# A four-layer graph network on one core: inverse norms brought back interleaved, diagonal blocks summed on VectorE, another order of the first loads

## The chip, the cores and the metric

The kernel runs on one core of a Trainium2 chip. The metric is the device time in microseconds (us) from the first to the last instruction of that core. The core has TensorE (PE, matrix products), VectorE (DVE), ScalarE (ACT), GpSimd (POOL) and SyncE (SP, which here issues nearly all DMA transfers). Each engine works through its own instructions in order; the engines wait for each other by semaphores.

## The reference, cut to what matters

There are 32 graphs (batches) of 512 nodes with 128 features, each with its own 512 x 512 weighted adjacency. Four layers follow each other, each on the normed nodes, each added to its input:

```python
h = relu(layernorm(x))
# layer 0: (adj + eye) scaled on both sides by degree ** -0.5
adj1 = adj + eye(512);  r = sum(adj1, -1) ** -0.5
x = x + leaky_relu((adj1 * r[:, :, None] * r[:, None, :]) @ (h @ W) + b)
# layer 1: adj @ elu(in), adj.T @ elu(out), elu(node), one update with tanh
# layer 2: four steps, each of them
src_agg = einsum('bjv,bij->biv', nodes @ ws + bs, l2norm(adj, 2))   # by rows of adj
dst_agg = einsum('bjv,bji->biv', nodes @ wd + bd, l2norm(adj, 1))   # by columns of adj
nodes = tanh(concat(src_agg, nodes @ wn + bn, dst_agg) @ wu + bu)   # steps 2, 3 also take earlier nodes
# layer 3: a gated recurrent unit on m = tanh(adj @ msg)
```

Everything is float32. The host lays `adj` and its transpose out by partition (`adj`, `adjt`), so that the kernel holds `a` and `aT`, each 128 partitions x 4 chunks x 512.

## The kernel before

The kernel does not issue its instructions as it meets them. It records every operation with its engine, an assumed duration and the buffers it reads and writes, and a planner (`Plan`) then lays them out in one fixed order for each engine, interleaving two or three batches, and assigns buffers from pools. Where the planner expects a hole in PE's work, it puts in small products (`ps_idle`) that keep PE's clock up; their results are not used. A line in the profile such as L350 is a helper that records matmuls, so its rows are told apart by tile names.

Loads wait in the planner as long as data is on a round trip through DRAM (`plan.way` opens at the first operation and closes at the last): "loads yield to turned rows". Only what stands in `FIRST` is exempt, and is issued in that order:

```python
TURN = 32
OWN = 2
FIRST = ["x0", "a0", "aT0", "c", "raw0", "w1", "r1", "raw2", "raw3", "x1", "a1", "aT1", "x2", "a2", "aT2"]
...
        def load(dst, src, kb, rank):
            name = f"{rank}{b}"
            rank, kb = first(name), kb * (2 if name == "a0" else 1)
            n = NC // pieces
            for k in range(pieces):
                s = slice(k * n, (k + 1) * n)
                op("SP", 0.4, lambda s=s: nc.sync.dma_start(dst.ap()[:, s, :], src[:, s, :]),
                   [], [(dst, set(range(NC)[s]))], kb=kb / pieces, rank=rank, yields=rank is None)
```

`raw0`, `raw2`, `raw3` are layer 2's raw weights, which the kernel multiplies into one another (`ps_fold`) before it uses them; `c` holds biases.

Layer 0 adds the unit matrix to the four diagonal 128 x 128 blocks of `aT`, into `diag`; the aggregation then takes `diag` for those blocks and `aT` for the rest. The sum is one instruction over all four blocks (one for each block in batch 0):

```python
        n = NC if b else 1
        own_engine, own_name = (nc.vector, "DVE") if b < OWN else (nc.gpsimd, "POOL")
        for k in range(0, NC, n):
            op(own_name, t_tt(n * P) if b < OWN else t_pool(n * P), lambda k=k, n=n: own(k, n), [(aT, set(range(k, k + n))), ID], [(diag, set(range(k, k + n)))])
```

Layer 2 needs each row and column of the adjacency divided by its norm. ACT sums squares along the free dimension into `stat` (128 x 8: four chunks of `a`, four of `aT`), POOL raises them to the power -0.5, and the 8 x 128 results must then stand along the free dimension, the same on all partitions, to be multiplied into `aT` and `a`:

```python
        root = op("POOL", t_pow(2 * NC), lambda: nc.gpsimd.tensor_tensor(inv.ap()[:, :2 * NC], stat.ap(), neg_half, op=ALU.pow), [stat, NH], [inv])
        bounce, rows = buf("bounce", (P, TURN)), buf("s4", (P, NC, 2, NC, TURN), "rows")
        op("DVE", 0.1, lambda: nc.vector.transpose(turned_inv.ap(), inv.ap()), [inv], [turned_inv])
        # bounced(): 128 x 32 from turned_inv to DRAM
        # spread():  from DRAM to all partitions, 4 runs of 256 words each
        op("SP", 0.4, bounced, [turned_inv], [bounce], kb=16)
        plan.way(root, op("SP", 0.4, spread, [bounce], [rows], kb=640))
        for s, m in enumerate((aT, a)):
            for c in range(NC):
                op("DVE", t_tt(N), lambda m=m, c=c, s=s: nc.vector.tensor_mul(
                    m.ap()[:, c, :].rearrange("p (k q r) -> p k q r", k=NC, q=NC), m.ap()[:, c, :].rearrange("p (k q r) -> p k q r", k=NC, q=NC),
                    rows.ap()[:, :, s].rearrange("p q c r -> p c q r")), [(m, {c}), rows], [(m, {c})])
```

The same DVE turning of 32 x 32 blocks, with a trip through DRAM (`turn_turned`, `turned`, `f4r`), turns node rows into columns in the middle batches; batches 0, 1 and 31 use PE for it.

Other names that the prediction uses: `h` is the normed node tile (four ACT ACTIVATEs), `hT` and `f` have features on partitions, `rep` holds layer 1's `elu` of `in` and `out`, `sd` layer 2's `src` and `dst` rows, `msg` layer 3's messages.

Of the kernel before, what the change touches and what calls it, by code (L numbers as in the profile page):

```python
# [13 lines left out]
F32 = mybir.dt.float32  # L14
AF = mybir.ActivationFunctionType
ALU = mybir.AluOpType
AX = mybir.AxisListType

P = 128
B, N, D = 32, 512, 128  # L20
NC = N // P
# [3 lines left out]
PERIOD = 28.0  # L25
ENDING = 6.0
SMALL = 16
TURN = 32
OWN = 2

FIRST = ["x0", "a0", "aT0", "c", "raw0", "w1", "r1", "raw2", "raw3", "x1", "a1", "aT1", "x2", "a2", "aT2"]


SEVEN = {"last": 0 * 5 * D, "mid": 1 * 5 * D, "gates": 2 * 5 * D}
# [242 lines left out]
def gnn_stack(  # L277
# [11 lines left out]
    nc = tc.nc  # L289
    const = ctx.enter_context(tc.tile_pool(name="const", bufs=1))  # L290
    sb = ctx.enter_context(tc.tile_pool(name="sb", bufs=1))
    psum = ctx.enter_context(tc.tile_pool(name="psum", bufs=1, space=bass.MemoryType.PSUM))
    dram = ctx.enter_context(tc.tile_pool(name="dram", bufs=1, space=bass.MemoryType.DRAM))
    plan = Plan(sb, psum, {"bank": 8, "s2": 33, "s4": 5, "s8": 10}, {"bank": 1, "s2": 5, "s4": 0, "s8": 1})

    w_sb = const.tile([P, W_COLS], F32, name="w_sb")
    c_sb = const.tile([P, C_COLS], F32, name="c_sb")
# [3 lines left out]
    t_sb = const.tile([P, T_COLS], F32, name="t_sb")  # L301
    cg_sb = const.tile([P, 4], F32, name="cg_sb")
    ident = const.tile([P, P], F32, name="ident")
    inv_sb = const.tile([P, 8, TURN], F32, name="inv_sb")
    neg_half = const.tile([P, 2 * NC], F32, name="neg_half")

    def wt(col, n=D):
# [9 lines left out]
    def t_tt(n, pointers=0):  # L317
        return 0.065 + 0.058 * pointers + n / 960
# [10 lines left out]
    def t_pow(n):  # L329
        return 0.35 + 0.157 * n  # L330

    def op(*args, **kwargs):
        return plan.op(*args, **kwargs)

    def first(name):
        return FIRST.index(name) if name in FIRST else None

    def const_buf(name, ap):
        b = Buf(plan, name, name, None)
        b.tile, b.slot = ap, 0  # L340
        return b

    W1, W2F, W3, CS, RS, RF, CF, TS, ID, NH, CG = (const_buf(n, t) for n, t in (
        ("w1", w_sb), ("w2", w_sb), ("w3", w_sb), ("c_sb", c_sb), ("r_sb", r_sb), ("rf_sb", rf_sb),
        ("cf_sb", cf_sb), ("t_sb", t_sb), ("ident", ident), ("neg_half", neg_half), ("cg_sb", cg_sb)))

    INV, INV_T = ([const_buf(f"inv{j}_{k}", inv_sb[:, 4 * j + k, :]) for k in range(4)] for j in range(2))

    def mm(ps, out_of, lhs, rhs, n, start, stop, reads, later=0.0):
        op("PE", t_mm(n), lambda: nc.tensor.matmul(out_of(ps.ap()), lhs(), rhs(), start=start, stop=stop),  # L350
           reads, [ps], later=later)
# [9 lines left out]
    def setup():  # L361
# [1 line left out]

        op("POOL", 1.0, lambda: make_identity(nc, ident), [], [ID])
        op("POOL", 0.2, lambda: nc.gpsimd.memset(neg_half, -0.5), [], [NH])
        op("POOL", 0.21, lambda: nc.gpsimd.memset(inv_sb, 0.0), [], INV + INV_T)
        first_l2 = W_L2[0][0]

        def spread(lo, hi, to=None):
# [21 lines left out]
        for i in (0, 2, 3):  # L391
            lo, hi = RAW_L2[i][0], RAW_L2[i + 1][0] if i == 2 else RAW_COLS if i == 3 else RAW_L2[2][0]
            buf = plan.buf("s8", (P, NC, N), f"raw{i}")
# [9 lines left out]
        for i, (k, (proj, upd)) in enumerate(zip(L2_CHUNKS, RAW_L2, strict=True)):  # L403
            part = [0, 2] * k + [1] * k
            buf = raws[i][0]
            for lo in range(0, 3 * k, NC):
                n = min(NC, 3 * k - lo)
# [41 lines left out]
    def program(b):  # L449
        plan.batch = b  # L450

        def buf(tag, shape=(P, N), name=None):
            return plan.buf(tag, shape, name)
# [68 lines left out]
        pieces = NC if b == 0 else 2  # L522

        def load(dst, src, kb, rank):


            name = f"{rank}{b}"
            rank, kb = first(name), kb * (2 if name == "a0" else 1)
            n = NC // pieces
            for k in range(pieces):  # L530
                s = slice(k * n, (k + 1) * n)
                op("SP", 0.4, lambda s=s: nc.sync.dma_start(dst.ap()[:, s, :], src[:, s, :]),
                   [], [(dst, set(range(NC)[s]))], kb=kb / pieces, rank=rank, yields=rank is None)
# [236 lines left out]
# [4 lines that stand above are left out]
        psh = plan.bank("agg")  # L774
# [17 lines left out]
        x1 = buf("s2", rows_shape, "xr")  # L792
# [3 lines left out]
        h1, _ = normed(x1, "h")  # L796
# [11 lines left out]
        for h in range(2):  # L808
            s, part, halves = slice(2 * h, 2 * h + 2), {2 * h, 2 * h + 1}, set(range(4 * h, 4 * h + 4))
# [19 lines left out]
        x2 = buf("s2", rows_shape, "xr")  # L829
# [3 lines left out]
        stat = buf("stat2", (P, 2 * NC))  # L833
        sq = buf("s2", name="sq")
        for c in range(NC):
            for s, m in ((0, a), (1, aT)):
                op("ACT", 0.73, lambda c=c, s=s, m=m: nc.scalar.activation(  # L837
                    sq.ap(), m.ap()[:, c, :], AF.Square, accum_out=stat.ap()[:, s * NC + c:s * NC + c + 1]), [(m, {c})], [sq, (stat, {s * NC + c})])
        inv, turned_inv = INV[b % len(INV)], INV_T[b % len(INV_T)]
        op("DVE", 0.08, lambda: nc.vector.tensor_scalar_max(stat.ap(), stat.ap(), NORM_EPS * NORM_EPS), [stat], [stat])  # L840
        root = op("POOL", t_pow(2 * NC), lambda: nc.gpsimd.tensor_tensor(inv.ap()[:, :2 * NC], stat.ap(), neg_half, op=ALU.pow), [stat, NH], [inv])  # L841


        bounce, rows = buf("bounce", (P, TURN)), buf("s4", (P, NC, 2, NC, TURN), "rows")
        op("DVE", 0.1, lambda: nc.vector.transpose(turned_inv.ap(), inv.ap()), [inv], [turned_inv])

        def bounced():
            bounce.tile = dram.tile([P, TURN], F32, name=f"bounce_{b}", tag=f"bounce_{bounce.slot}", bufs=1)
            nc.sync.dma_start(bounce.tile, turned_inv.ap())

        def spread():
            d = bounce.tile
            nc.sync.dma_start(rows.ap().rearrange("p q s c r -> p q (s c r)"),
                              bass.AP(tensor=d.tensor, offset=d.offset, ap=[[0, P], [TURN * TURN, NC], [1, 2 * P]]))

        op("SP", 0.4, bounced, [turned_inv], [bounce], kb=16)

        plan.way(root, op("SP", 0.4, spread, [bounce], [rows], kb=640))
        for s, m in enumerate((aT, a)):
            for c in range(NC):  # L860
                op("DVE", t_tt(N), lambda m=m, c=c, s=s: nc.vector.tensor_mul(  # L861
                    m.ap()[:, c, :].rearrange("p (k q r) -> p k q r", k=NC, q=NC), m.ap()[:, c, :].rearrange("p (k q r) -> p k q r", k=NC, q=NC),
                    rows.ap()[:, :, s].rearrange("p q c r -> p c q r")), [(m, {c}), rows], [(m, {c})])


        h2, _ = normed(x2, "h")
        f0 = transposed(h2, "f0")
        f, stashed = [f0], [f0]
# [4 lines left out]
        for i, (wsd, wn) in enumerate(W_L2):  # L873
# [11 lines left out]
            for h, o in order:  # L885
                m, lo = ((aT, 0), (a, D))[o]
# [10 lines left out]
            f = {0: [f_new], 1: [f_new, stashed[1]], 2: [f_new, stashed[1], stashed[0]], 3: [f_new]}[i]  # L897
# [14 lines left out]
        h3, _ = normed(x3, "h")  # L912
# [6 lines left out]
        aT2 = buf("s8", (P, NC, N), "aT2")  # L919
# [40 lines left out]
        u, n, q, w, xo = (buf("s2", rows_shape, k) for k in ("u", "n", "q", "w", "xo"))  # L960
        side, side_engine = (nc.gpsimd, "POOL") if at_end else (nc.vector, "DVE")
        w1 = 1 if at_end else 2
        for k in range(0, NC, w1):
            s, part, cols = slice(k, k + w1), set(range(k, k + w1)), 2 * D * w1
# [3 lines left out]
        for k in range(0, NC, w2):  # L968
            s, part, cols = slice(k, k + w2), set(range(k, k + w2)), w2 * D
# [71 lines left out]
```

## Time and profile before

| | before |
|---|---|
| device time, median of 3 runs | 2325.16 us (2324.03 to 2326.28) |
| span of the profiled run | 2322.2 us |
| busy: PE, DVE, ACT, POOL | 2301.4, 1529.8, 870.7, 261.8 us |
| granted PE clock | 1.000 |
| moved by DMA | 201.23 MB, 87 GB/s on average |

In the profile's rows, a group is one line, engine, operation and tile; after the bar stand its busy time, the mean duration of one instruction in ns, and the idle time of the engine ahead of the group with what ended it. Each float32 product is shown as two matmul records (two passes). Ends of matmuls are modelled, and successive matmuls overlap.

### The profile page before, as it was taken

How to read it: one execution, taken by the hardware profiler on the slowest of the kernel's cores; microseconds unless marked ns; L12 is line 12 of the kernel's file. 1: busy time of each engine (PE TensorE's matmuls, PEld its weight loads, DVE VectorE, ACT ScalarE, POOL GpSimd, SP SyncE). 2: the span in 40 equal slices, each digit the busy share in tenths (PEclk: the TensorE clock that was granted, in tenths of full speed). 3: DMA queues.
4: the chain of work that ended last, by engine and by line, in shares of the span. 5: the costliest groups of instructions: out<-in, count | busy, mean ns of one | idle time of the engine just before them, and what ended most of it. 6: DMA issues, size and time to landing. Idle time of an engine off the chain costs nothing.

```text
span 2322.2 us, 28292 instructions
## 1 busy us (share of the span) xinstructions
PE 2301.4 (99%) x9662; PEld 1442.0 (62%) x9662; DVE 1529.8 (66%) x4179; ACT 870.7 (37%) x1970; POOL 261.8 (11%) x210
## 2 busy tenths in 40 slices
PE   9999999999999999999999999999999999999999
PEld 7566666666666666666666656666666666566666
DVE  7646666676666766667666667666676666676655
ACT  7313433343333443334433334333344333343322
POOL 3001110111101111101101011110111110111101
PEclk9999999999999999999999999999999999999999
DMA  7102312323223323233232232322332222323201
GB/s 261 28 28 64 121 56 87 109 87 105 64 83 99 110 82 87 69 91 109 83 102 62 83 109 87 105 64 82 100 110 82 87 68 93 109 83 105 69 10 32
DMA packets 145056, 201.23 MB, mean 87 GB/s; under 512 B 18960, under 2 KB 96016, under 8 KB 144912
## 3 DMA queue, kind: packets, MB, share of 16 engines
q1 hardware_dynamic: 144624, 199.30, 27.9%
q8 instruction: 76, 1.25, 0.2%
q14 instruction: 68, 0.56, 0.1%
q10 hardware_dynamic: 288, 0.13, 0.0%
HBM read 160.05 MB, written 39.32 MB: 86 GB/s over the span
## 4 chain that ended last, share of the span: by engine, by line
PE 73%; DMA 10%; DVE 8%; POOL 3%; SPq 3%; ACT 2%; issue 1%; ACTq 0%; POOLq 0%; DVEq 0%
PE ps_agg L350 49%; PE ps_seven L716 9%; PE ps_sd L350 8%; DMA x<-in_x 4%; DMA turn_turned<-blk 3%; PE ps_gate L350 3%; PE ps_upd L350 2%; POOL sc L584 2%; SPq L614 2%; DVE bn L542 2%; PE ps_lin L350 1%; ACT h L596 1%; DVE sd L672 1%; POOL inv_sb L841 1%; DVE aT L861 1%
## 5 line engine op out<-in xcount | busy, mean ns | idle before, releaser
L350 PE MATMUL ps_agg<-aT,sd 128*128 128x512 f32 x1024 | 503.8, 593 | 0.1
L350 PE MATMUL ps_agg<-a,sd 128*128 128x512 f32 x1024 | 502.0, 593 | 0.0
L584 POOL TENSOR_TENSOR sc<-v,neg_half 128x4 f32<-128x4 f32 (+1 forms) x127 | 163.1, 1284 | 981.9 <-DVE v L759 489.9
L596 ACT ACTIVATE h<-xr,nb,sc 128x128 f32<-128x128 f32 x384 | 158.2, 482 | 277.3 <-DVE nb L592 277.2
L350 PEld LDWEIGHTS ps_agg<-aT,sd 128*128 128x128 f32 x1024 | 179.8, 191 | 109.6 <-issue 96.1
L350 PEld LDWEIGHTS ps_agg<-a,sd 128*128 128x128 f32 x1024 | 175.9, 191 | 114.8 <-issue 112.9
L350 PE MATMUL ps_agg<-f,w_sb 128*128 128x512 f32 x448 | 229.0, 593 | 0.4 <-ACT f L891 0.4
L716 PEld LDWEIGHTS ps_seven<-t_sb,s 128*128 128x128 f32 x1128 | 167.3, 191 | 92.6 <-issue 84.9
L350 PE MATMUL ps_sd<-w_sb,f 128*128 128x256 f32 x768 | 219.5, 380 | 0.5 <-ACT f L891 0.3
L965 ACT ACTIVATE g<-g 128x512 f32<-128x512 f32 (+1 forms) x64 | 36.1, 609 | 396.3 <-DVE g L694 395.8
L350 PEld LDWEIGHTS ps_sd<-w_sb,f 128*128 128x128 f32 x768 | 132.8, 191 | 79.8 <-issue 51.5
L716 PE MATMUL ps_seven<-t_sb,s 128*128 128x128 f32 x1128 | 178.6, 275 | 0.0
L672 DVE TENSOR_TENSOR sd<-ps_sd,rf_sb 128x512 f32<-128x512 f32 x128 | 87.8, 686 | 97.6 <-PE ps_sd L350 97.5
L742 DVE TENSOR_TENSOR ev<-ps_seven,ev 128x512 f32<-128x512 f32 x94 | 64.9, 691 | 131.7 <-PE ps_seven L716 131.4
L350 PE MATMUL ps_agg<-aT,msg 128*128 128x512 f32 (+1 forms) x264 | 132.0, 585 | 5.8 <-DVE msg L917 5.7
L350 PE MATMUL ps_agg<-aT,rep 128*128 128x512 f32 x256 | 131.0, 593 | 3.2 <-DVE rep L813 3.2
L350 PE MATMUL ps_agg<-a,rep 128*128 128x512 f32 x256 | 130.7, 592 | 0.0
L841 POOL TENSOR_TENSOR inv_sb<-stat,neg_half 128x8 f32<-128x8 f32 x32 | 53.0, 1657 | 672.3 <-DVE stat L840 648.8
L891 ACT ACTIVATE f<-ps_agg,cf_sb 128x512 f32<-128x512 f32 x128 | 87.3, 682 | 103.3 <-PE ps_agg L350 100.8
L716 PEld LDWEIGHTS ps_seven<-w_sb,f 128*128 128x128 f32 x512 | 80.4, 191 | 50.2 <-issue 47.3
L350 PE MATMUL ps_agg<-aT,h 128*128 128x256 f32 (+2 forms) x384 | 99.6, 381 | 0.6 <-ACT h L569 0.6
L837 ACT ACTIVATE sq<-aT 128x512 f32<-128x512 f32 x128 | 80.1, 626 | 51.0 <-DMA aT<-in_adjt 49.9
(175 smaller groups left out, 3781.0 us busy)
## 6 DMA issues: line engine op xcount, KB each, us to landing
aT<-in_adjt SPq DMA_DIRECT2D x124, 512.0 KB, 6.7
a<-in_adj SPq DMA_DIRECT2D x62, 512.0 KB, 5.7
turn_turned<-blk SPq DMA_DIRECT2D x348, 64.0 KB, 2.3
turned<-turn_turned SPq DMA_DIRECT2D x87, 256.0 KB, 2.7
rows<-bounce SPq DMA_DIRECT2D x32, 512.0 KB, 5.1
x<-in_x SPq DMA_DIRECT2D x32, 256.0 KB, 6.9
out<-xo SPq DMA_DIRECT2D x30, 256.0 KB, 2.0
turn_f4r<-blk SPq DMA_DIRECT2D x116, 64.0 KB, 1.8
```

The costliest lines, as they stand in the source:

```text
L350: op("PE", t_mm(n), lambda: nc.tensor.matmul(out_of(ps.ap()), lhs(), rhs(), start=start, stop=stop), reads, [ps], later=later)
L542: op("DVE", 0.193, lambda c=c: nc.vector.bn_stats(st.ap()[:, c, :], xin.ap()[:, c, :]), [xin], [(st, {c})])
L584: op("POOL", t_pow(n), lambda: nc.gpsimd.tensor_tensor(inv.ap()[:, :n], v8.ap()[:, :n], neg_half[:, :n], op=ALU.pow), [v8, NH], [(inv, {0})])
L596: op("ACT", t_act(D, 2), lambda c=c: nc.scalar.activation(h.ap()[:, c, :], xin.ap()[:, c, :], AF.Relu, bias=nb.ap()[:, c:c + 1], scale=inv ...
L614: nc.sync.dma_start(bounce.tile[:, k, :].rearrange("(b s) n -> s b n", b=NC), blk.ap()[k * P // NC:(k + 1) * P // NC])
L672: op("DVE", t_tt(N), lambda ps=ps, h=h: nc.vector.tensor_add(sd.ap()[:, 2 * h:2 * h + 2, :], ps.ap().rearrange("p (j v) -> p j v", j=2), s ...
L716: op("PE", t_mm(D), lambda j=j: nc.tensor.matmul(ps.ap()[:, k * H + j * D:k * H + (j + 1) * D], lhs()[:, j * P:(j + 1) * P], rhs(), start= ...
L742: op("DVE", t_tt(N), lambda: nc.vector.tensor_add(ev.ap(), bank_b.ap()[:, None, :H].to_broadcast([P, 2, H]), ev.ap()), [bank_b, ev], [ev])
L837: op("ACT", 0.73, lambda c=c, s=s, m=m: nc.scalar.activation(sq.ap(), m.ap()[:, c, :], AF.Square, accum_out=stat.ap()[:, s * NC + c:s * NC ...
L841: root = op("POOL", t_pow(2 * NC), lambda: nc.gpsimd.tensor_tensor(inv.ap()[:, :2 * NC], stat.ap(), neg_half, op=ALU.pow), [stat, NH], [inv])
L891: op("ACT", t_act(N, 1), lambda ps=ps, i=i, f_new=f_new: nc.scalar.activation(f_new.ap(), ps.ap(), AF.Tanh, bias=cf_sb[:, i:i + 1]), [ps, ...
L965: op("ACT", t_act(cols), lambda s=s: nc.scalar.activation(g.ap()[:, s, :2 * D], g.ap()[:, s, :2 * D], AF.Tanh, scale=0.5), [(g, fields(par ...
```

## The change

The rows of inverse norms take another way: the 128 x 8 block goes to DRAM as POOL leaves it, one transfer brings its 1024 words to every partition in the order in which they lie (node, then statistic), and ACT copies them into rows, reading every eighth word. DVE's turn, its zeroed constant tile and the four-dimensional views of the multiplications go away. The diagonal block sums of all batches are recorded for VectorE. The loads that are exempt from yielding are fewer: the bias block and `raw0` stand ahead of `aT0`, and batches 1 and 2 are no longer in the list. The pool of small buffers has 32 in place of 33, that of the next size 6 in place of 5. The purpose is a simpler path for the rows, less work on GpSimd, and loads of later batches that give way.

```diff
-TURN = 32
-OWN = 2
-FIRST = ["x0", "a0", "aT0", "c", "raw0", "w1", "r1", "raw2", "raw3", "x1", "a1", "aT1", "x2", "a2", "aT2"]
+OWN = 32
+FIRST = ["x0", "a0", "c", "raw0", "aT0", "w1", "r1", "raw2", "raw3"]
...
-    plan = Plan(sb, psum, {"bank": 8, "s2": 33, "s4": 5, "s8": 10}, ...)
+    plan = Plan(sb, psum, {"bank": 8, "s2": 32, "s4": 6, "s8": 10}, ...)
...
-        op("POOL", 0.21, lambda: nc.gpsimd.memset(inv_sb, 0.0), [], INV + INV_T)
...
-            name = f"{rank}{b}"
-            rank, kb = first(name), kb * (2 if name == "a0" else 1)
+            rank = first(f"{rank}{b}")
...
-        bounce, rows = buf("bounce", (P, TURN)), buf("s4", (P, NC, 2, NC, TURN), "rows")
-        op("DVE", 0.1, lambda: nc.vector.transpose(turned_inv.ap(), inv.ap()), [inv], [turned_inv])
+        bounce, spaced, rows = buf("bounce", (P, 2 * NC)), buf("s4", (P, P, 2 * NC), "spaced"), buf("s4", (P, 2, N), "rows")
...
-            nc.sync.dma_start(rows.ap().rearrange("p q s c r -> p q (s c r)"),
-                              bass.AP(tensor=d.tensor, offset=d.offset, ap=[[0, P], [TURN * TURN, NC], [1, 2 * P]]))
-        op("SP", 0.4, bounced, [turned_inv], [bounce], kb=16)
-        plan.way(root, op("SP", 0.4, spread, [bounce], [rows], kb=640))
+            nc.sync.dma_start(spaced.ap().rearrange("p n k -> p (n k)"),
+                              bass.AP(tensor=d.tensor, offset=d.offset, ap=[[0, P], [1, 2 * N]]))
+        op("SP", 0.4, bounced, [inv], [bounce], kb=128)
+        plan.way(inv.uses[0][0], op("SP", 0.4, spread, [bounce], [spaced], kb=512))
+        op("ACT", 1.97, lambda: nc.scalar.copy(
+            rows.ap().rearrange("p s (c n) -> p (s c) n", c=NC), spaced.ap().rearrange("p n k -> p k n")), [spaced], [rows])
         for s, m in enumerate((aT, a)):
             for c in range(NC):
-                op("DVE", t_tt(N), lambda m=m, c=c, s=s: nc.vector.tensor_mul(... four-dimensional views ...), [(m, {c}), rows], [(m, {c})])
+                op("DVE", t_tt(N), lambda m=m, c=c, s=s: nc.vector.tensor_mul(m.ap()[:, c, :], m.ap()[:, c, :], rows.ap()[:, s, :]),
+                   [(m, {c}), rows], [(m, {c})])
```

The planner lays out all of this anew, so the order on each engine changes in many places beyond the lines above.

## The prediction

> **What bounds the kernel now.** I read the engine table first, then the stretches of the span, the waits of TensorE (PE), the timeline of the first 46 us and the groups by form.
>
> ```profile
> PE 2301.4 (99%) x9662; PEld 1442.0 (62%) x9662; DVE 1529.8 (66%) x4179; ACT 870.7 (37%) x1970; POOL 261.8 (11%) x210
> ```
>
> PE is busy for 2301.4 of 2322.2 us. That share cannot be taken at its word, because matmuls overlap. The Trainium skill says so in "Perfetto Trace Analysis", section "Identifying the Most-Contended Engine", and this trace agrees: one 128x512 product is shown at 593 ns, but eight in a row take 3.60 us.
>
> ```profile
> 2289.85 3.60 PE L350 MATMUL ps_agg<-aT,sd 128*128 128x512 f32 x8
> 2295.86 1.05 PE L350 MATMUL ps_msg<-w_sb,hT 128*128 128x128 f32 x8
> 2288.99 1.03 PE L350 MATMUL ps_sd<-w_sb,f 128*128 128x256 f32 x4
> ```
>
> So the step from one product to the next is (3.60 - 0.593) / 7 = 0.430 us for 512 columns, (1.05 - 0.275) / 7 = 0.111 for 128, and (1.03 - 0.380) / 3 = 0.217 for 256. The groups by form hold about 3322, 5000 and 1204 of these, and 128 of 384 columns (0.324 in between). 3322 x 0.430 + 5000 x 0.111 + 1204 x 0.217 + 128 x 0.324 = 2286 us; less the 86 products that only keep PE's clock up (86 x 0.111 = 10), 2276 us. That is PE's floor, about 71.1 us for each of the 32 batches. The kernel loses 2322 - 2276 = 46 us, 2.0% of its time. Where, the view of six stretches tells (stretch, its length, then the busy time of PE, PEld, DVE, ACT, POOL, each with its instructions; last PE's clock, the DMA share and GB/s):
>
> ```profile
> 0.00:30.00 30.00, 27.40 (x194) 25.17 (x194) 15.53 (x78) 19.08 (x47) 8.75 (x16) 1.00 0.95 352
> 30.00:80.00 50.00, 47.70 (x181) 28.64 (x182) 37.80 (x126) 33.43 (x91) 11.46 (x9) 1.00 0.43 124
> ...
> 230.00:2170.00 1940.00, 1930.18 (x8049) 1202.20 (x8048) 1302.48 (x3527) 741.02 (x1671) 220.93 (x165) 1.00 0.29 90
> 2170.00:2225.00 55.00, 52.03 (x218) 32.43 (x217) 34.73 (x92) 19.35 (x41) 6.06 (x5) 1.00 0.17 53
> 2225.00:2322.00 97.00, 94.09 (x401) 60.66 (x400) 51.47 (x131) 21.01 (x48) 5.96 (x10) 1.00 0.07 20
> ```
>
> The steady part, 27 batches, has 1940 - 1930 = 10 us of visible gaps: 0.36 us a batch. The rest lies in the start (no real product before 9.87 us, keep-warm products up to 30 us) and in the end. DVE has a third of its time free, ACT almost two thirds, POOL nine tenths. What engines other than PE do counts only where PE waits for it.
>
> The waits of PE confirm it; these are the largest of nine, in all under 17 us:
>
> ```profile
> PE ps_agg L350 <- DVE msg L917: 5.7, 10, 1.0
> PE ps_agg L350 <- DVE rep L813: 3.2, 2, 2.5
> PE ps_sd L350 <- ACT hT L638: 3.1, 4, 1.1
> ```
>
> **The change part by part.** (1) The rows of inverse norms. Before, POOL's 128x8 result is turned by DVE, goes to DRAM and comes back as rows. After, the 128x8 block goes to DRAM as it is, comes back to every partition as one run of 4 KB with the eight statistics interleaved, and a new ACT copy puts them in order. Removed: 32 turns on DVE and a memset.
>
> ```profile
> L845 DVE STREAM_TRANSPOSE inv_sb<-inv_sb 128x32 f32<-128x32 f32 x32 | 6.7, 209 | 15.6 <-POOL inv_sb L841 15.6
> L768 POOL TENSOR_TENSOR diag<-aT,ident 128x512 f32<-128x512 f32 x30 | 38.5, 1284 | 383.5 <-DMA aT<-in_adjt 370.1 <-PE ps_sd L350 13.4
> L768 DVE TENSOR_TENSOR diag<-aT,ident 128x512 f32<-128x512 f32 x1 | 0.7, 674 | 0.0
> ```
>
> Added: 32 ACT copies of 128x1024. ACT's slope comes from this trace: 128x256 from PSUM with a pointer took 474 ns and 128x512 took 687, so 0.83 ns an element; from a 128x512 copy at 617 ns I get 617 + 512 x 0.83 = 1042 ns for 1024 elements side by side. But the copy reads every eighth word, 32 bytes apart. "SBUF — State Buffer", section "Door 1: The DMA port swizzle", says that SBUF has 16-byte lines and that each access that crosses to a new line pays a penalty; here each element does. No instruction of this trace reads so, and the page gives no factor. I take up to twice, about 2 us. 32 x 2 = 64 us raise ACT from 871 to 935 us, 40%. The transfer's 512 KB stay, in pieces four times as large; the way back took 5.1 us before, and I expect 4.5 to 5. So the chain from POOL's power to usable rows becomes about 2 us longer for the copy and 0.2 us (plus a hand-over) shorter for the turn.
>
> In the steady part this hides: in the batch I followed, the rows were issued at 1056.9 us, landed about 1062, and the first multiplication that uses them ran at 1071.8. That is 10 us of slack against 2. The danger is the place of the copy in ACT's own order. In the built program it stands ahead of a layer norm's four ACTIVATEs, so if the rows land later than the order assumes, ACT stands still with the norm behind it. One or two us of that, in some batches, can reach PE through the turned rows.
>
> (2) The diagonal blocks of batches 2 to 31 go from POOL to DVE. DVE gains 30 x 0.674 = 20.2 us and loses 6.7: 1530 to 1543 us, still 66%. POOL loses 38.5. "GPSIMD Engine Reference", section "4.1 Engine selection", puts two-input elementwise work at about twice VectorE's time on GpSimd; here 1284 / 674 = 1.9. Both engines work beside PE, so I book 0 for it. On DVE, which runs in order, a block whose adjacency lands late would hold up everything behind it; in the built program it stands after the gate sums, at a place where the trace before has `aT` landed over 10 us earlier. Again 0.
>
> (3) The order of the first loads. Before, `aT0` follows `a0` at once, and the loads of batches 1 and 2 come ahead of the first bounce. After, the small bias block and 768 KB of raw weights come between, and the loads of batch 2 after the first rows. The DMA moves 352 GB/s in the first 30 us, so 0.79 MB / 352 GB/s = 2.2 us of delay for `aT0`. Its blocks were needed at 9.43 us, and the last of the first aggregation's products ran at 14.2, set partly by the `h` chunks (the last ready at 13.4), so about 1 us of the 2.2 reaches the chain. The folds of layer 2's weights are now ahead of the first linear products and fill the hole, but do not shorten the chain.
>
> ```profile
> 22.98 8.43 DMA bounce<-inv_sb
> 31.43 6.55 DMA rows<-bounce
> ```
>
> These two steps of the chain of waits (start, length) go the other way: the first 16 KB bounce took 8.4 us against 1.4 in the steady part, behind 9.9 MB of loads. "DMA: Bandwidth & Descriptors", section "Queues, rings and completion order", says that descriptors are consumed in ring order on each DMA engine, which fits. After, about 7.4 MB stand ahead, and the bounce should take 2 to 4 us. But in the new order of ACT the first reordering copy stands between the two exponentials that make `rep` for layer 1 of batch 0, where PE has nothing else:
>
> ```profile
> 28.27 1.37 ACT L810 ACTIVATE rep<-sd 128x512 f32<-128x512 f32 x2 [0.71 <-DVE sd L672]
> 30.50 1.12 PE L350 MATMUL ps_agg<-aT,rep 128*128 128x512 f32 x2 [0.68 <-DVE rep L813]
> ```
>
> The second exponential now comes behind the rows' landing (some 29 to 31 us by the numbers above) and 2 us of copy. The first half of `rep` feeds four instructions of two passes each, 8 x 0.430 = 3.4 us, which covers most of this. I book 1 to 2 us.
>
> (4) The counts. The built programs' instruction lists hold 4857 and 4863 PE instructions, of which 43 and 49 keep the clock up: 4814 of the real kind in both. So PE's floor of 2276 us does not move; six more fillers of two passes are 12 x 0.111 = 1.3 us, spent in holes of the start. One buffer of a large kind replaces a small one; the end has the same order of engines and loads, and I book 0 there.
>
> Sum: +1 (first aggregation) +1.5 (first `rep`) +1 (fillers and reordering at the start) +2 (steady part, 0.05 to 0.1 us a batch for the copy's place) = about +5 us: 2325 + 5 = 2330 us.
>
> **The rivals.** *The copy and the block sums break the steady rhythm.* If each batch lost another 0.5 us, the 30 batches would lose 15: 2340 us. For it: ACT and DVE run in order and the copy waits for a DMA. Against it: 10 us of slack, and PE had only 10 us of gaps in 1940 although DVE already stood still for `x` 28 times, 46 us in all. *The old order was worse than it looks.* The first rows came late in the old kernel, on the chain that ended last; with rows at 32 instead of 38 us, the start could be 3 us shorter than before, and with POOL free of the blocks its powers could come earlier: 2320 us. Against it: batch 2's loads come later, and PE's only gap there over 1 us waited for a layer norm, not for rows. *DVE or ACT becomes the bound:* at 66% and 40% this is out of the question.
>
> **Range and chances.** The gain cannot exceed the 46 us lost now, and most of that is the unavoidable ramp, so faster by 2% has 1 chance in 100. Slower by 2% needs 46 us more, 1.5 us a batch; 1 in 100. The range of 8 in 10 runs from 2319 (the second rival) to 2343 us (the first, a little beyond), around 2330.
>
> **What would show it.** PE's sum less fillers stays the same; the steady part's period stays within 71.3 to 71.8 us; the ACT copy shows 1.7 to 2.3 us; the first bounce lands in under 5 us; the first product on `diag` comes 1 to 3 us later than 9.87; the first product on `rep` at 31 to 33 us; the block sums on DVE at about 0.67 us with no wait for DMA. It would be wrong if PE shows new waits in each batch (for `hT`, `msg` or `rep`) adding to over 15 us, or if the start becomes shorter.

## The result and the profile after

| | before | after |
|---|---|---|
| device time, median of 6 runs each | 2324.6 us (2323.67 to 2326.28) | 2314.95 us (2313.66 to 2315.88) |
| ratio after / before, 95% interval | | 0.9957 (0.9944 to 0.9970) |
| span of the profiled run | 2322.2 us | 2313.0 us |
| busy: PE, DVE, ACT, POOL | 2301.4, 1529.8, 870.7, 261.8 us | 2300.9, 1548.1, 928.7, 224.2 us |

The changed kernel is faster by 0.43%. The prediction said 2330 us, with a range of 2319 to 2343: it is wrong, and in direction too. The engine table of after:

```profile
PE 2300.9 (99%) x9674; PEld 1451.0 (63%) x9674; DVE 1548.1 (67%) x4177; ACT 928.7 (40%) x2002; POOL 224.2 (10%) x179
```

The table hides the gain: PE is busy for the same time in a span that is 9 us shorter. The stretches of after show more (stretch, length, busy time and instructions of PE, PEld, DVE, ACT, POOL; PE's clock, DMA share, GB/s):

```profile
0.00:30.00 30.00, 26.35 (x175) 24.72 (x176) 14.80 (x74) 18.72 (x49) 8.32 (x15) 0.94 0.87 296
30.00:80.00 50.00, 47.86 (x204) 30.30 (x203) 35.89 (x124) 38.75 (x90) 11.53 (x8) 1.00 0.43 157
230.00:2160.00 1930.00, 1928.26 (x8064) 1209.91 (x8063) 1321.30 (x3534) 784.80 (x1685) 184.05 (x136) 1.00 0.29 90
2160.00:2215.00 55.00, 53.54 (x222) 33.10 (x222) 36.69 (x97) 26.72 (x58) 7.21 (x5) 1.00 0.22 69
2215.00:2313.00 98.00, 94.87 (x404) 61.16 (x402) 51.69 (x131) 21.10 (x48) 5.97 (x10) 1.00 0.07 19
```

The same stretch of before:

```profile
230.00:2160.00 1930.00, 1920.18 (x8009) 1195.88 (x8008) 1296.89 (x3515) 738.36 (x1665) 219.86 (x164) 1.00 0.29 89
```

In 1930 us, PE's visible gaps fell from 9.8 to 1.7 us, and it completed 8064 records where it had completed 8009, 0.7% more. That is 55 x 1930 / 8064 = 13 us worth of work, more than the 8 us of gaps: the rest of the loss had been counted as busy.

The output transfers, one for each batch, divide the 9.2 us between the spans. From the issue of the third to that of the thirtieth 1929.2 us passed before and 1916.4 after: 12.9 us gained, 0.48 a batch. The third itself was issued at 334.41 before and at 338.05 after: 3.6 us lost in the start. From the thirtieth to the end both took 58.6 us. So the start became longer, as predicted, the end did not move, and the gain is all in the steady part, where I had booked a loss of 2.

What PE waited for, after (the three largest):

```profile
PE ps_agg L346 <- DVE diag L761: 2.2, 1, 2.2
PE ps_agg L346 <- DVE rep L806: 1.5, 2, 1.2
PE ps_sd L346 <- ACT hT L631: 1.4, 3, 0.6
```

Against before, the 5.7 us for `msg` are gone and those for `hT` halved; the first two rows belong to the start. More of it stands where I had not looked, in the waits of PE's weight loads and of ACT. First before, then after (us, times, longest):

```profile
ACT hT L638 <- DMA turned<-turn_turned: 112.3, 30, 7.3
PEld ps_agg L350 <- DVE msg L917: 22.7, 28, 1.8
PEld ps_sd L350 <- ACT hT L638: 22.5, 27, 1.9
```
```profile
ACT hT L631 <- DMA turned<-turn_turned: 57.1, 49, 7.2
PEld ps_sd L346 <- ACT hT L631: 3.0, 8, 0.8
PEld ps_agg L346 <- DVE msg L907: 0.3, 1, 0.3
```

ACT's wait for turned rows halved, and what PE's loads waited for behind it, 45 us, fell to 3. So the turned rows come back sooner, although no line of the change touches them. The list of DMA issues says how (number, KB, median us from issue to landing), before and after:

```profile
turn_turned<-blk SPq DMA_DIRECT2D x348, 64.0 KB, 2.3
...
rows<-bounce SPq DMA_DIRECT2D x32, 512.0 KB, 5.1
```
```profile
turn_turned<-blk SPq DMA_DIRECT2D x348, 64.0 KB, 1.8
...
spaced<-bounce SPq DMA_DIRECT2D x32, 512.0 KB, 4.3
```

And one batch on the DMA queue shows where the two meet. Before, and then after (start, us, what is issued):

```profile
1055.42 0.34 SPq L849 DMA_DIRECT2D bounce<-inv_sb  x1
1056.86 0.37 SPq L853 DMA_DIRECT2D rows<-bounce  x1
1058.78 1.77 SPq L614 DMA_DIRECT2D turn_turned<-blk  x4
1062.74 0.34 SPq L618 DMA_DIRECT2D turned<-turn_turned  x1
```
```profile
1054.58 0.32 SPq L843 DMA_DIRECT2D spaced<-bounce  x1
1057.30 1.79 SPq L607 DMA_DIRECT2D turn_turned<-blk  x4
1060.51 0.34 SPq L611 DMA_DIRECT2D turned<-turn_turned  x1
```

`turned` can be issued only once the four parts of `turn_turned` have landed. Before, they are issued 1.9 us behind a transfer that needs 5.1 us, and `turned` follows 3.96 us after the first of them; after, 3.21. Call this time, from the first `turn_turned` behind the rows to the issue of `turned`, the *first trip*. Its mean over the 27 steady batches is 4.10 us before and 3.46 after. It is not the same in all batches: after, two of three take 3.15 to 3.4 us and most of the third ones 3.6 to 4.6.

The new parts cost what was expected of them (groups by form, after):

```profile
L848 ACT COPY rows<-spaced 128x1024 f32<-128x1024 f32 x32 | 66.4, 2075 | 24.1 <-DMA spaced<-bounce 23.7
...
L761 DVE TENSOR_TENSOR diag<-aT,ident 128x512 f32<-128x512 f32 x31 | 21.1, 682 | 1.6 <-DMA aT<-in_adjt 1.6
```

### The profile page after: what moved, and what is told of

It is laid out like the page before. It is cut to its first block, busy times and chain, and to the rows that moved or that the text cites. A ratio compares the mean times of both kernels' runs of the same rounds, so it can differ in the third digit from the quotient of the medians.

```text
span 2313.0 us, 28274 instructions
## 1 busy us (share of the span) xinstructions
PE 2300.9 (99%) x9674; PEld 1451.0 (63%) x9674; DVE 1548.1 (67%) x4177; ACT 928.7 (40%) x2002; POOL 224.2 (10%) x179
## 4 chain that ended last, share of the span: by engine, by line
PE 93%; DMA 3%; DVE 2%; ACT 1%; POOL 1%; issue 0%; SPq 0%; DVEq 0%; ACTq 0%; POOLq 0%
PE ps_agg L346 62%; PE ps_seven L709 12%; PE ps_sd L346 9%; PE ps_upd L346 3%; PE ps_gate L346 3%; PE ps_msg L346 1%; PE ps_lin L346 1%; PE ps_node L346 1%; DMA spaced<-bounce 1%; DMA aT<-in_adjt 1%; DMA bounce<-inv 1%; POOL inv L834 0%; ACT rows L848 0%; POOL sc L577 0%; ACT h L589 0%; DVE z L781 0%
## 5 line engine op out<-in xcount | busy, mean ns | idle before, releaser
L577 POOL TENSOR_TENSOR sc<-v,neg_half 128x4 f32<-128x4 f32 (+1 forms) x127 | 152.1, 1198 | 1479.1 <-DVE v L538 977.4
L750 ACT ACTIVATE sq<-a 128x512 f32<-128x512 f32 x124 | 77.5, 625 | 114.0 <-DMA a<-in_adj 112.2
L834 POOL TENSOR_TENSOR inv<-stat,neg_half 128x8 f32<-128x8 f32 x32 | 64.3, 2008 | 587.2 <-DVE stat L833 587.2
L598 DVE STREAM_TRANSPOSE blk<-h 128x512 f32<-128x512 f32 x87 | 61.6, 708 | 74.2 <-ACT h L589 74.2
L852 DVE TENSOR_TENSOR a<-a,rows 128x512 f32<-128x512 f32 x128 | 87.8, 686 | 11.7 <-PE ps_agg L346 11.6
```

The costliest lines, as they stand in the source:

```text
L577: op("POOL", t_pow(n), lambda: nc.gpsimd.tensor_tensor(inv.ap()[:, :n], v8.ap()[:, :n], neg_half[:, :n], op=ALU.pow), [v8, NH], [(inv, {0})])
L598: op("DVE", t_tt(N), lambda: nc.vector.transpose(blk.ap().rearrange("p b (c r) -> p c b r", c=NC), m.ap().rearrange("p c (b s) -> p c b s" ...
L750: op("ACT", 0.73, lambda c=c: nc.scalar.activation(sq.ap(), a.ap()[:, c, :], AF.Copy, accum_out=stat.ap()[:, c:c + 1]), [(a, {c})], [sq, ( ...
```

## The experiments

Times are medians; ratios are to the kernel before, measured beside it (2323 to 2325 us), with 95% intervals.

### Which part of the change gains?

In the changed kernel `x` is issued ahead of `a` and lands in 2.9 us in place of 6.9, so DVE's wait for it fell from 46 to 4 us. Theory A: this place of the loads gains. Theory B: the rows path gains.

**e1: the diagonal sums alone.**

```diff
-OWN = 2
+OWN = 32
```

> The old kernel with one thing changed: the diagonal block sums of batches 2 to 31 on VectorE. In its built order the loads have already moved: x, a, aT now follow the third round trip of turned rows instead of the second, and x stands ahead of a. Theory A (the gain of the steady part comes from where the loads fall, which the block sums' engine decides): the steady part runs at 70.75 us a batch instead of 71.3, DVE's wait for x falls from 46 us to under 6, and with the old start the time is 2311 us (-12 to -14). Theory B (the gain comes from the new path of the rows): no change, 2322 to 2327 us, and the gain shows in e2.

2323.03 us, ratio 0.9992 (0.9984 to 1.0001). The planner moves `x` ahead of `a` here too, `x` lands in 3.0 us and DVE's wait for it falls to 6 us, but the time stays. Theory A falls, and the engine of the block sums is worth nothing by itself. Two signs of the last section fall with it: in e1 `turn_turned` lands in 1.8 us and ACT's wait for turned rows is 59 us, both as after, without any gain. The first trip, 4.12 us in e1, is still that of before.

**e2: the rows path alone** (kernel before, with the change's hunks on rows and pools).

```diff
-        bounce, rows = buf("bounce", (P, TURN)), buf("s4", (P, NC, 2, NC, TURN), "rows")
+        bounce, spaced, rows = buf("bounce", (P, 2 * NC)), buf("s4", (P, P, 2 * NC), "spaced"), buf("s4", (P, 2, N), "rows")
... (spread, ACT copy, flat multiplications, pools 32 and 6, as in the change)
```

> The old kernel with the rows' new path alone (bounce of the 128x8 block, one 4 KB run to each partition, ACT copy; pools 32 and 6). In its built order the loads stand as in the old kernel. Theory A: the steady part stays at 71.3 us a batch, DVE still waits about 46 us for x; 2323 to 2329 us. Theory B: 2313 to 2316 us.

2310.04 us, ratio 0.9935 (0.9920 to 0.9950): more than the whole gain. `spaced` lands in 3.6 us, and the first trip takes 3.35. `x` still lands late (DVE waits 25 us for it), so theory B holds without A.

**e3: the first loads alone.**

```diff
-FIRST = ["x0", "a0", "aT0", "c", "raw0", "w1", "r1", "raw2", "raw3", "x1", "a1", "aT1", "x2", "a2", "aT2"]
+FIRST = ["x0", "a0", "c", "raw0", "aT0", "w1", "r1", "raw2", "raw3"]
-            rank, kb = first(name), kb * (2 if name == "a0" else 1)
+            rank = first(name)
```

> The old kernel with the new order of the first loads alone. Both theories: the first real product 2 us later, the first product on rep 1 to 3 us later, the steady part as before: 2326 to 2330 us, +2 to +5. If the start costs nothing, the loss of 4 us that the new kernel shows in its first 180 us comes from the ACT copy.

2332.66 us, ratio 1.0038 (1.0025 to 1.0051), above the range expected. The third output transfer is issued 5.8 us later than before; the rest, 3.3 us, is lost at 0.12 us a batch.

**e4: the change without its first loads** (the lines of e3 the other way, on the changed kernel).

> The new kernel with the old order of the first loads. Theory A and B alike: the new steady part with the old start, 2310 to 2312 us, about 4 us below the new kernel. If the rows' path itself costs or brings nothing, it equals e1.

2310.49 us, ratio 0.9936 (0.9919 to 0.9952). The changed kernel pays about 4.5 us for its first loads (the kernel before paid 8 in e3), of which 4.0 are there by the third output transfer. And e4 differs from e2 only in the block sums' engine: again nothing.

### What about the rows path?

The old transfer brings each partition four runs of 1 KB that lie 4 KB apart in DRAM (the turned block is 128 rows of 128 bytes; for each of its four groups of 32 rows, the first 8 are wanted). The new one brings one run of 4 KB. But DVE's turn, the planner's order, its assumed sizes and the pools change as well.

**e5: kernel before, the bounce permuted in DRAM, so that each partition reads one run.** No ACT copy; the order of the instructions on every engine is that of before. `rows` lies flat here, so the multiplications use the flat views (681 and 676 ns each, 679 and 674 before).

```diff
-            nc.sync.dma_start(bounce.tile, turned_inv.ap())
+            d = bounce.tile
+            nc.sync.dma_start(bass.AP(tensor=d.tensor, offset=d.offset, ap=[[TURN, NC], [P, TURN], [1, TURN]]), turned_inv.ap())
...
-                              bass.AP(tensor=d.tensor, offset=d.offset, ap=[[0, P], [TURN * TURN, NC], [1, 2 * P]]))
+                              bass.AP(tensor=d.tensor, offset=d.offset, ap=[[0, P], [1, 2 * N]]))
```

> The kernel before, in its own order of instructions on every engine; only the addresses of the bounce differ: DVE's turned block is written to DRAM so that the 1024 words stand as (statistic, node), and each partition reads them as one run of 4 KB in place of four of 1 KB. No ACT copy. Theory 'run size' (the old transfer of 5.1 us in 1 KB runs stands in the way of the first turned rows of each batch): rows land in 3.6 to 4.3 us, turn_turned in 1.8 in place of 2.3, ACT's wait for hT <- turned falls from 112 us to below 60, and the time is 2308 to 2314 us. Theory 'order' (the planner's new order gains, not the transfer): 2323 to 2326. Theory 'turn' (DVE's turn, which stands still for POOL, is what costs): 2323 to 2326.

2308.61 us, ratio 0.9942 (0.9927 to 0.9956). The whole gain, with neither ACT copy nor new order: the transfer is what counts. ACT's wait for turned rows fell only to 99 us, not below 60, so that number was no good sign; the first trip (3.61 us) is a better one.

**e6: e2 with four runs of 1 KB again**, 2 KB apart.

```diff
-            nc.sync.dma_start(bounce.tile, inv.ap())
+            nc.sync.dma_start(bass.AP(tensor=d.tensor, offset=d.offset, ap=[[4 * P, NC], [2 * NC, 32], [1, 2 * NC]]), inv.ap())
-                              bass.AP(tensor=d.tensor, offset=d.offset, ap=[[0, P], [1, 2 * N]]))
+                              bass.AP(tensor=d.tensor, offset=d.offset, ap=[[0, P], [4 * P, NC], [1, 2 * P]]))
```

> The rows path alone as in e2 (2310 us), in e2's own order, but the interleaved block lies in DRAM in four pieces of 1 KB with gaps between, so that each partition gets four runs of 1 KB again. Theory 'run size': spaced lands in about 5 us in place of 3.6, turn_turned takes 2.3 again, and the time goes back to 2320 to 2326 us. Theories 'order' and 'turn': it stays at 2308 to 2313.

2312.27 us, ratio 0.9954 (0.9938 to 0.9970); landing 4.0 us. The size of the runs was my theory, and it falls: 144673 packets, nearly as many as before (145056), but hardly slower than e2 with 132769.

**e7: only the assumed sizes.**

```diff
-        op("SP", 0.4, bounced, [turned_inv], [bounce], kb=16)
+        op("SP", 0.4, bounced, [turned_inv], [bounce], kb=128)
-        plan.way(root, op("SP", 0.4, spread, [bounce], [rows], kb=640))
+        plan.way(root, op("SP", 0.4, spread, [bounce], [rows], kb=512))
```

> The kernel before with nothing changed but the sizes that the planner assumes for the two transfers (128 and 512 KB in place of 16 and 640), which shifts the order of instructions a little. Theory 'order': 2310 to 2318 us. Theories 'run size' and 'turn': 2322 to 2327.

2322.75 us, ratio 1.0000 (0.9992 to 1.0009). Nothing.

**e8: e2 with the old pools.**

```diff
-    plan = Plan(sb, psum, {"bank": 8, "s2": 32, "s4": 6, "s8": 10}, ...)
+    plan = Plan(sb, psum, {"bank": 8, "s2": 33, "s4": 5, "s8": 10}, ...)
```

> The rows path alone as in e2 (2310 us), with the pools of the kernel before (33 small buffers and 5 of the next size, in place of 32 and 6). If the larger pool is what gains: 2318 to 2326 us. If it is the transfer or the turn: 2308 to 2314.

2311.97 us, ratio 0.9957 (0.9940 to 0.9974). The pools are not it either.

### The distance between the runs

e5 and e6 leave one thing that sets them apart from before: where the runs lie.

**e9: kernel before, its four 1 KB runs 5 KB apart in place of 4.** Same order on every engine, and 144672 packets.

```diff
-            bounce.tile = dram.tile([P, TURN], ...)
+            bounce.tile = dram.tile([P, TURN + 8], ...)
-            nc.sync.dma_start(bounce.tile, turned_inv.ap())
+            nc.sync.dma_start(bass.AP(tensor=d.tensor, offset=d.offset, ap=[[TURN * (TURN + 8), NC], [TURN, TURN], [1, TURN]]), turned_inv.ap())
-                              ... ap=[[0, P], [TURN * TURN, NC], [1, 2 * P]]))
+                              ... ap=[[0, P], [TURN * (TURN + 8), NC], [1, 2 * P]]))
```

> The kernel before in its own order, with its four 1 KB runs for each partition; but the four runs lie 5 KB apart in DRAM in place of 4 KB. e6 (1 KB runs, 2 KB apart) landed in 4.0 us and e5 (one 4 KB run) in 3.8, against 5.1 before (4 KB apart), so size of run alone did not explain it. Theory 'distance of 4 KB is slow': rows land in about 4 us and the time is 2308 to 2314 us. Theory 'short runs are slow when written in 128 B pieces' (as before and e5 write them, unlike e6): landing 5.1, 2322 to 2326 us.

2309.35 us, ratio 0.9935 (0.9918 to 0.9953), landing 4.0 us. A distance of 5 KB gives the whole gain. One batch of e9 on the DMA queue:

```profile
1046.77 0.54 SPq L850 DMA_DIRECT2D bounce<-inv_sb  x1
1048.73 0.39 SPq L854 DMA_DIRECT2D rows<-bounce  x1
1050.13 1.81 SPq L614 DMA_DIRECT2D turn_turned<-blk  x4
1053.92 0.34 SPq L618 DMA_DIRECT2D turned<-turn_turned  x1
```

**e10: e6 with the runs 4 KB apart** (`4 * P` becomes `8 * P` in the lines of e6).

> e6 (rows path of the change, 1 KB runs, 2312 us) with the runs 4 KB apart in DRAM in place of 2 KB. Theory 'distance of 4 KB is slow': spaced lands in about 5 us, turn_turned in 2.2 to 2.3, and the time goes to 2319 to 2326 us. Theory 'order or ACT copy gains': 2310 to 2314 us, whatever the landing.

2332.58 us, ratio 1.0038 (1.0024 to 1.0052), landing 5.2 us. The changed rows path loses its gain, and more, as soon as its runs lie 4 KB apart. The queue in e10:

```profile
1060.14 0.39 SPq L845 DMA_DIRECT2D spaced<-bounce  x1
1061.80 1.75 SPq L608 DMA_DIRECT2D turn_turned<-blk  x4
1066.01 0.34 SPq L612 DMA_DIRECT2D turned<-turn_turned  x1
```

The first trip is 4.21 us here against 3.79 in e9, behind gaps of 1.66 and 1.40: the wider gap has the longer trip. In e6, which differs from e10 by the distance alone (and the size of the DRAM tile), PE and its weight loads waited 5.7 us for `hT`; in e10 they waited 39.9.

**e11: e5 with 256 KB more in the way**, DRAM to DRAM, which nobody waits for.

```diff
+        def spread_and_more():
+            spread()
+            more = dram.tile([P, 512], F32, name=f"more_{b}", tag=f"more_{b % 4}", bufs=1)
+            nc.sync.dma_start(more, adj[0][:, 0, :])
```

> e5 (2308.6 us) with one more transfer right behind the rows in each batch: 256 KB from DRAM to DRAM, which nobody waits for. It only occupies the DMA engines ahead of the first turned rows. Theory 'collision' (a batch pays for what stands ahead of its first turn_turned): that transfer's landing rises from 2.1 to above 2.5 us, ACT waits longer for hT <- turned, and the time goes to 2315 to 2330 us. Rival 'late rows' (the rows' own landing is what is paid for): 2308 to 2311 us.

2329.1 us, ratio 1.0025 (1.0017 to 1.0033). About 20 us are lost. The trace has no landing times for these transfers, but it shows no wait for `rows`. The waits of PE's loads, e5 and then e11:

```profile
PEld ps_sd L350 <- ACT hT L638: 10.9, 26, 1.7
```
```profile
PEld ps_sd L350 <- ACT hT L638: 30.1, 27, 2.4
```

With PE's own waits these are 12.4 and 37.5 us. So a batch pays for what stands ahead of its first turned rows, not for the rows' own arrival.

**e12: e5 with the way back issued behind the second trip** (the issue is moved in the finished order, nothing else).

```diff
+        out = self.rows_later(out)   # rows<-bounce behind the second turned<-turn_turned that follows it
```

> e5 with the bounce's way back issued behind the second turned-row trip of its batch, ahead of the loads of a; the other engines' orders stay as they are. The rows were needed some 15 us after their old issue, and the second trip ends about 10 us after it, so they land just in time or a fraction late. Theory 'collision': turn_turned lands in 1.8 in place of 2.1, and the time is 2304 to 2308 us if the rows come in time; DVE's wait for rows shows what is lost if not. Rival 'late rows': 2309 to 2318 us.

2323.37 us, ratio 1.0002 (0.9992 to 1.0011): neither theory's number. The first trip did shorten, to 3.34 us, and DVE waited only 3.7 us for rows. But `x` is now issued 1.4 us behind the rows (in one batch near 1066 us), and DVE's wait for it rose from 25 us in e5 to 58. PE's loads show where that ends:

```profile
PEld ps_agg L359 <- DVE msg L929: 33.2, 28, 1.8
```

With PE's own waits, 46.0 us for `msg` and 5.7 for `hT`, against 13.3 and 12.4 in e5. The chain that ended last runs through the landing of `x` for 6% of the span in e12, 1% in e5 and 4% before. So the collision was moved, not removed, and the rows' transfer can cost in two places: at the first turned rows, and at `x` behind them. The waits tell where, not how much: in e1 they are only 18.3 us for `hT` and 0.7 for `msg`, against 25.6 and 28.4 before, at the same time.

**e15 and e16: kernel before with the runs 8 KB, and 4 KB + 128 bytes apart** (`TURN + 8` of e9 becomes `2 * TURN`; in e16 the DRAM tile stays that of e9, and only the distance becomes `TURN * (TURN + 1)`).

> The kernel before in its own order with its four 1 KB runs 8 KB apart in DRAM in place of 4 KB. e9 with 5 KB was 2309 us, landing 4.0. If distances that are multiples of 4 KB are slow: rows land in 5 us or more, 2322 to 2335 us. If only 4 KB itself is, or if what matters is that all runs lie in one small region: about 4 us and 2308 to 2312.

> The same with the runs 4 KB + 128 B apart. If exact multiples of 4 KB are slow because the runs then begin at the same place of a 4 KB block: 128 bytes leave most of each 1 KB run at the same places, so the landing stays near 5 us and the time at 2320 to 2325. If it is the exact distance: about 4 us and 2308 to 2312.

2470.71 us, ratio 1.0623 (1.0604 to 1.0642), and 2340.31 us, ratio 1.0068 (1.0053 to 1.0083). The DMA lists of e15 and e16:

```profile
rows<-bounce SPq DMA_DIRECT2D x32, 512.0 KB, 8.2
```
```profile
rows<-bounce SPq DMA_DIRECT2D x32, 512.0 KB, 5.0
```

So 128 bytes more do not help, 1 KB more does, and 8 KB is far worse: the 512 KB that landed in 4.0 us need 8.2. Both times are above all ranges expected. In e15 the granted clock fell as well, to 0.972; at that clock PE's 70.7 us a batch would be 72.7, so by this estimate up to 2 of the 5 us that a batch of e15 loses may be the clock's.

One batch of e16, to be set beside that of e9:

```profile
1062.42 0.39 SPq L854 DMA_DIRECT2D rows<-bounce  x1
1063.82 1.78 SPq L614 DMA_DIRECT2D turn_turned<-blk  x4
1068.36 0.34 SPq L618 DMA_DIRECT2D turned<-turn_turned  x1
```

The gap is 1.40 us in both, the trip 4.54 us here and 3.79 there. All together (first trip: mean of the 27 steady batches, from the queue's issues as above):

| way back of the rows | landing, us | first trip, us | time, us |
|---|---|---|---|
| e5: one run, order of before | 3.8 | 3.61 | 2308.6 |
| e9: four runs 5 KB apart, order of before | 4.0 | 3.72 | 2309.4 |
| before: 4 KB apart | 5.1 | 4.10 | 2324.6 |
| e16: 4 KB + 128 B apart | 5.0 | 4.71 | 2340.3 |
| e15: 8 KB apart | 8.2 | 7.44 | 2470.7 |
| e11: e5 and 256 KB behind it | | 4.42 | 2329.1 |
| e12: e5, rows behind the second trip | 4.7 | 3.34 | 2323.4 |
| e1: 4 KB apart, block sums | 5.3 | 4.12 | 2323.0 |
| e2: one run, new path | 3.6 | 3.35 | 2310.0 |
| e6: four runs 2 KB apart, new path | 4.0 | 3.45 | 2312.3 |
| e10: four runs 4 KB apart, new path | 5.2 | 4.43 | 2332.6 |
| after: one run, new path, block sums, first loads | 4.3 | 3.46 | 2315.0 |
| e13, e14: after, with half of its first loads undone | 4.2, 4.3 | 3.74, 3.77 | 2324.5, 2322.5 |

Two pairs differ only in where the runs lie. From e16 to e9, with the same DRAM tile and the same form of the write, the trip shrinks by 0.99 us and the time by 31, over 28 batches 1.1 each; from e10 to e6 by 0.98 us and 20, 0.7 each. From before to e9 it is 0.38 us and 15, but there the write differs too: e9 and e16 write the bounce by a view of three dimensions, and issue the way back 1.94 us behind it, before 1.48 (means of the steady batches). So the turned rows of e16 follow its rows at a gap of 1.46 us, those of before at 1.94, which would make the trip longer at the same landing. The first trip alone does not give the time: e12 has a short one and e13 that of e9, and both are 14 to 15 us slower than e9 (e13 by 6 of them in its start). From before to e9, PE and its loads waited 25.6 and 14.1 us for `hT`, 28.4 and 16.6 for `msg`: the gain is in both places.

The Trainium skill has the effect on a larger scale, in "DMA: Bandwidth & Descriptors", section "Latency and other measured facts": rows at a pitch of 2 MiB or more copied at less than the full rate, a padding of a few KiB restored it, and 192 bytes did not. It calls the cause, streams that meet in one memory channel, an inference. These runs agree in kind, at distances of only 4 and 8 KB; they do not show the cause either.

### What do the first loads cost?

**e13 and e14: the changed kernel with one half of its first loads undone each.**

```diff
-FIRST = ["x0", "a0", "c", "raw0", "aT0", "w1", "r1", "raw2", "raw3"]
+FIRST = ["x0", "a0", "aT0", "c", "raw0", "w1", "r1", "raw2", "raw3"]                                              # e13
+FIRST = ["x0", "a0", "c", "raw0", "aT0", "w1", "r1", "raw2", "raw3", "x1", "a1", "aT1", "x2", "a2", "aT2"]   # e14
```

> The changed kernel (2315 us) with one part of its new first loads undone: aT0 stands behind a0 at once again, ahead of the biases and raw0; batches 1 and 2 still yield. Theory 'the late aT0 is what the new first loads cost': the first product on diag comes at about 10 us in place of 11.9, the first linear product at 16.3 in place of 18.4, and the time is 2311 to 2313 us. Rival 'the loads of batches 1 and 2, and ACT's copy between the two halves of rep, are what costs': 2314 to 2316.

> The changed kernel (2315 us) with the other part undone: the loads of batches 1 and 2 are exempt from yielding again; aT0 still stands behind the biases and raw0. Theory 'the late aT0 costs': 2314 to 2316 us. Rival 'batches 1 and 2 cost': 2310 to 2313 us, the first product on rep at about 31 to 33 us in place of 34.

2324.51 us, ratio 1.0001 (0.9992 to 1.0010), and 2322.52 us, ratio 0.9991 (0.9983 to 1.0000). Both theories fail. In the start neither half brings anything back: the third output transfer is issued at 338.85 and 338.56 us, against 338.05 in after and 334.05 in e4. In e13 the early `aT0` is of no use because the planner, for which `a0` no longer counts double, now puts a sum of squares of `aT` on ACT ahead of the normed nodes, and the first product waits for those until 11.95 us. Each half alone brings none of the 4 us that both together bring.

Beyond that they lose 9 and 8 us between the third and the thirtieth, although beyond the first batches every engine has the same order of instructions as in after. In e13 two batches are quick, the third slow. A slow one, and the next:

```profile
1203.18 1.91 SPq L607 DMA_DIRECT2D turn_turned<-blk  x4
1208.39 0.34 SPq L611 DMA_DIRECT2D turned<-turn_turned  x1
...
1275.67 1.77 SPq L607 DMA_DIRECT2D turn_turned<-blk  x4
1278.84 0.34 SPq L611 DMA_DIRECT2D turned<-turn_turned  x1
```

Both stand 2.7 us behind their `spaced`, yet one trip takes 5.2 us and the other 3.2, and such a batch takes 72.2 to 72.5 us in place of 70.8. It is the first trip again, but in this batch not behind the rows' transfer: `spaced` had landed 3.5 us behind its issue, at about 1204.0, while the parts were still being issued, and of the four parts of `turn_turned` three landed in 1.7 to 1.9 us, and one, from the order of issues the last, needed 3.6. After has the long trip in one of three batches too (3.6 to 4.6 us), but there the parts are issued only 1.4 to 1.9 us behind `spaced`, not 2.7, so the way back is hardly later. What makes that one part slow was not found.

## Why the prediction was wrong, point by point

- **What bounds the kernel: right, but the room was too small.** PE is the bound in both kernels. My 71.1 us a batch, an average over all 32, was no floor for the steady ones: after, most take 70.7 to 70.8. The visible gaps (0.36 us a batch) were half of what could be gained, since waits inside overlapping matmuls count as busy.
- **Step 1, the rows path: this step failed.** It said "The transfer's 512 KB stay, in pieces four times as large; the way back took 5.1 us before, and I expect 4.5 to 5", then "In the steady part this hides", and booked +2 us. The landing of 4.3 and the copy of 2075 ns (1.7 to 2.3 expected) were near enough, and the 10 us of slack were there. But I asked only when the rows are needed. What the runs put in its place: the transfer stands on the DMA engines ahead of the batch's first turned rows, and these PE does wait for (and for `x`, which comes behind them): e9 is 31 us quicker than e16 by the distance of the runs alone, and 15 us quicker than before; e11 loses 20 by 256 KB that nobody reads. The term of +2 measured -14.4 (e2). The pieces' size, which I had named, matters little (e6); what I had passed over was that they lay 4 KB apart.
- **Step 2, the block sums: right.** Booked 0, measured 0 within the noise (e1 against before, e4 against e2), at 682 ns each; the only waits for `aT` are in the start.
- **Step 3, the first loads: right in kind, 1 us too small in the changed kernel.** The first product on `diag` came at 11.86 us (1 to 3 us late was said, 2.0 measured), the bounce was quick (2.0 us from issue to that of `spaced`), the first product on `rep` came at 33.99, a microsecond past the range given. But of the 2.2 us by which `aT0` is late I let 1 reach the chain; the first linear product is 2.1 us late (18.42 us, 16.30 in e4). The lateness of `aT0` is not all of that: behind the 2.2 us in which PE waited for `diag`, the granted clock (third number from the end) fell. After, and then e13, whose first product came at 11.95 us:

```profile
14.00:16.00 2.00, 2.00 (x8) 1.69 (x7) 0.00 (x0) 1.25 (x4) 0.00 (x0) 0.50 1.04 419
```
```profile
14.00:16.00 2.00, 2.00 (x15) 1.70 (x14) 0.00 (x0) 1.91 (x7) 0.00 (x0) 1.00 1.04 421
```

In e13 the first linear product came at 17.06 us. So with the first product at nearly the same time, 1.4 us are lost where the clock was low. Why it fell in one and not in the other is open. Booked +2.5, and +1 for fillers and reordering; e4 measures 4.5, but e3, on the kernel before, 8.
- **Step 4, the counts: right.** 9674 records against 9662 are the fillers.
- **The rivals.** "The copy and block sums break the steady rhythm" is refuted: 0.48 us a batch were won, not lost. "The old order was worse than it looks" had the right sign by a wrong road: the start it counted on became longer. The sum with measured terms is -14.4 for the rows, 0 for the sums, +4.5 for the first loads: -9.9 us, against -9.65 measured. As the +4.5 is after less e4, this says only that e4 and e2 take the same time; the 8 us of e3 show that the terms do not simply add.

## What to carry to other kernels

For every transfer ask not only when its data is needed, but which transfer stands behind it in the queue and who waits for that one: a transfer with 10 us of slack of its own cost 15 us. Where many partitions read the same few pieces of a small DRAM buffer, keep them side by side, or try another distance than 4 or 8 KB (5 KB was quick, 4 KB + 128 bytes was not); in e9 one padding did all that a new path, an ACT copy and a new order were to do. And the change's gain was not that of its plan: undoing its first loads (e4), or the padding alone (e9), beats it by 4 to 6 us.

## What was unexpected of the hardware

- 512 KB, read by 128 partitions as the same four 1 KB runs, landed in 4.0 us with 2 or 5 KB between their starts, in 5.1 to 5.3 with 4 KB, in 5.0 with 4 KB + 128 bytes and in 8.2 with 8 KB. Runs of 1 KB as such cost little: 4.0 us against 3.8 (order of before) or 3.6 (new path) for one run of 4 KB.
- ACT's copy of 128x1024 with a source stride of 32 bytes took 2075 ns, twice the 1042 estimated for elements side by side. The 16-byte lines that the prediction cited fit that; no run here reads with another stride to test it.
- Programs with the same order on all engines beyond the first batches differ by 0.3 us a batch, in a pattern of three batches (e13 and e14 against after).
- The granted PE clock was 0.50 from 14 to 16 us in after and 1.00 in e13, although PE had stood still for about 2 us ahead of its first product in both. In e15, where PE waited most, the mean was 0.972.
